# A four-layer graph network on one core: edge searches issued further ahead, and one relational layer's projections cut into small steps

## The chip, the core and the metric

The kernel runs on one core of one Trainium2 chip. Its engines have queues of their own: PE multiplies matrices (with weight loads, PEld, beside it), DVE and ACT work element by element, POOL (GpSimd) here issues gathers, stores and index patterns, SP issues DMAs; ACT can issue DMAs too. An engine executes its queue in order. The metric is the device time of one execution in microseconds.

## The reference

3125 nodes with 128 features, 100,000 edges sorted by target (`dst`), each with a source and one of 8 types. Four networks follow one another; each result is added to its input and normalised by rows.

```python
# L0, three times: D^-1/2 (A + I) D^-1/2 h W, + b, layernorm, relu
deg = segment_sum(ones, row) ; dinv = rsqrt(deg) ; w = dinv[row] * dinv[col]
h = segment_sum(w[:, None] * (h @ W)[col], row) + b
# L1:  segment_sum((x @ W.T + b)[src], dst), own node included
# L2:  (1 + eps) x + segment_sum(x[src], dst), then two linear layers with batchnorm and relu
# L3, two relational layers (128 -> 256 -> 128), relu between:
h = einsum('ni,rio->rno', x, W)
msg = h[etype, src]
sums = segment_sum(msg, dst * 8 + etype) ; cnt = the same of ones
out = (sums / max(cnt, 1)).sum over types + x @ W_root + b
```

## The kernel before

The nodes are 25 blocks of 128. `listed` is the path that runs; `general` stands behind a flag for inputs with too many edges in a node and does not run here. The code is written for a planner that gives each engine its instructions in the order of their place in the program where nothing hinders it, and lets later work go ahead where earlier work still waits by its own estimate; so a line can run long before its place (L309's memset at 1.5 us). Semaphores and the reuse of buffers follow from the tiles: a tile with `bufs=2` makes the third user wait for the first.

**Edges and adjacency (L168 to L301).** Targets, sources and types are loaded as 125 partitions of 800 (L170). Every 200th target is loaded by itself into `smp` (L173), spread over all partitions by a product with ones (L192) and kept in `smb` (L194). The targets as floats go to `dsf` (L181) as 500 rows of 200; source, type and target are packed into one word (`w`, L183 and L185) and go to `pk` (L188). `search(s)` finds for 256 nodes where their edges begin: a coarse count over the samples (L212), a gather `g` of the row of 200 targets (L219), a fine count in it (L224), pointers `ptr` (L228). `keys(s)` gathers 64 packed words for each node (`ew`, L234), splits them (L239 to L249), and transposes them into `kT`. `total(b)` builds one block of the adjacency matrix in four units `u`: one-hot matrices `lo` and `hi` (L161, DVE), sixteen small products into `bld` (L271), an eviction by ACT into `at` (L273). After the four units the identity is added (L277, DVE), `at` is stored to `adj_t` (L278, SP), transposed in four groups through the PSUM tag `mi` (L283), evicted into `av` (L284, ACT), stored to `adj` (L286), and summed over sources by a product with a one-column `onesb` (L290) into two PSUM rows. The loop is written so: `search(0), search(1), keys(0)`, then for each s `search(s+2), keys(s+1), total(2s), total(2s+1)`.

**Passage.** The row sums are copied one row at a time (L312), transposed (L314), and their inverse root is `dinv` (L318 to L322). Then `begin` and `held` (a check) follow. Features `xa` and weights are loaded from the ACT queue, the first network's in a pool that reuses the memory of the edge stage (L473 to L495).

**First network.** `product` (L525 on) runs over seven chunks `CH` of 3 or 4 blocks; in each, five groups of five blocks are loaded (`m`, L514, SP) and multiplied with three bf16 parts of the features (L534). After each group `fill(1.3)` (L536) takes 1.3 steps from the generator `relations()` (L342 on), which counts edges by type (L347, L348, in one step), loads the inverse counts out, gathers the packed words of blocks 14 to 24 edge by edge (`gedge`, L376), makes the indices `gsrc` and keys `gkey` for them, and builds the per-type matrices `rel` of blocks 0 to 13 (56 units of two steps, L429, L448, L455, L457, stores L462 by POOL). A chunk ends with `done`: `times` (L587), bias, layernorm and the split for the next product on DVE and ACT. The second and third network (L569) follow.

**Relational layers.** Blocks 0 to 13 (`DENSE`, four chunks) are done by products with the matrices `rel`: `relation(r, m0, nb, ...)` loads five groups `m8` (L759), casts them (L767 ACT, L769 DVE) and multiplies (L772). After each group, 2.2 steps are taken from `gathered`, which does blocks 14 to 24 edge by edge: a tile of 128 edges is gathered by POOL (`gx`, L806, twelve buffers), one-hot keys `oh` are made by DVE (L798), and three short products per tile add into `ga` (L814); a block has 34 tiles, the last 15: 355. `put` then scales `ga` by the inverse counts. In the first layer `put1` (L875) writes into `z`, and when the chunk of `CH` is complete, `linear1` is called as a whole: transposes (L846), eight products of type weights and a root product for each of two halves (L852, L854), relu by ACT (L855), then for each block two groups of eight products with the second layer's weights (L862), each of which `store3` splits into three bf16 parts (ACT and DVE, L743 to L748) and stores to `ht_d`. `linear1` is also called at the end of each dense chunk. The second layer (L892 on) fetches `ht_d` and works in the same way without `linear1`.

```python
            ahead[0] = -14
            for m0, nb in DENSE:
                z = zp.tile([P, R, 512], F32, name="z", bufs=2)
                for r in range(R):
                    inv = load_inv(r, m0, nb)
                    acc = relation(r, m0, nb, xs, work, 2.2, (0, 1, 0, 1, 0))
                    nc.vector.tensor_mul(z[:, r, : nb * P], acc, inv)
                linear1(z, m0, nb)
            for _ in work:
                pass
```

Of the kernel before, what the change touches and what calls it, by code (L numbers as in the profile page):

```python
# [21 lines left out]
P = 128  # L22
# [4 lines left out]
R = 8  # L27
# [45 lines left out]
def listed(ctx: ExitStack, tc: tile.TileContext, p: dict, out: bass.AP, bad):  # L73
# [11 lines left out]
    onesb = const.tile([P, 1], BF, name="onesb")  # L85
# [5 lines left out]

    def column(name, n=1):
        t = const.tile([P, n], F32, name=f"c_{name}")
        with nc.allow_non_contiguous_dma(reason="a bias"):
            nc.scalar.dma_start(t, p[name].rearrange("(n p) -> p n", p=P))
        return t
# [51 lines left out]
    with ExitStack() as lists, tc.tile_pool(name="f_ps", bufs=1, space=PSUM) as psum:  # L148
# [6 lines left out]
        begin = bg.tile([P, SB, 2], F32, name="begin")  # L155

# [9 lines left out]
        with tc.tile_pool(name="f_t1", bufs=1) as t1:  # L166

            ei = [t1.tile([EP, ET], I32, name=f"e_{n}") for n in ("dst", "src", "edge_type_8")]  # L168
            for t, name in zip(ei, ("dst", "src", "edge_type_8")):
                nc.sync.dma_start(t, p[name].rearrange("(p t) -> p t", p=EP))  # L170
            smp = t1.tile([1, 500], I32, name="smp")
            with nc.allow_non_contiguous_dma(reason="every 200th edge"):
                nc.scalar.dma_start(smp, p["dst"].rearrange("(o i j) -> o i j", o=1, j=200)[:, :, 0])  # L173
# [3 lines left out]
            smf = t1.tile([1, 500], F32, name="smf")  # L177
            nc.vector.tensor_copy(smf, smp)
            df = t1.tile([EP, ET], F32, name="df")
            nc.vector.tensor_copy(df, ei[0])  # L180
            nc.sync.dma_start(dsf.rearrange("(p a) c -> p (a c)", p=EP), df)  # L181
            w = t1.tile([EP, ET], I32, name="w0")
            nc.vector.scalar_tensor_tensor(w, ei[2], 12, ei[1], op0=OP.logical_shift_left, op1=OP.bitwise_or)  # L183
            w2 = t1.tile([EP, ET], I32, name="w1")
            nc.vector.scalar_tensor_tensor(w2, ei[0], 15, w, op0=OP.logical_shift_left, op1=OP.bitwise_or)  # L185
            none = t1.tile([GM, P], I32, name="none")
            nc.vector.memset(none, -1)
            nc.sync.dma_start(pk[:E].rearrange("(p t) o -> p (t o)", p=EP), w2)  # L188
            nc.sync.dma_start(pk[E:].rearrange("(o t) c -> o (t c)", o=GM), none)

            t = psum.tile([P, 512], F32, name="mi", tag="mi", bufs=2)
            nc.tensor.matmul(t[:, :500], ones[0:1, :], smf, start=True, stop=True)  # L192
            smb = t1.tile([P, 500], F32, name="smb")
            nc.scalar.copy(smb, t[:, :500])  # L194
# [9 lines left out]
            fine = t1.tile([P, NC2], F32, name="fine")  # L204
            ptr = t1.tile([P, NC2], I32, name="ptr")
            valid = t1.tile([P, NC2, SL], BF, name="valid")

            def search(s):
# [7 lines left out]
                nc.vector.tensor_copy(irow[:, own], crow[:, own])  # L216
                for c in (2 * s, 2 * s + 1):
# [4 lines left out]
                    )  # L222
                    junk = t1.tile([P, 500], BF, name="junk", bufs=2)
# [6 lines left out]
            def keys(s):  # L230
                own = slice(2 * s, 2 * s + 2)
                ew = t1.tile([P, 2, SL], I32, name="ew", bufs=3)
                for i in range(2):
# [3 lines left out]
                    )  # L237
                f = [t1.tile([P, 2, SL], I32, name=f"f{i}", bufs=2) for i in range(4)]
# [20 lines left out]
            row = [psum.tile([P, 512], F32, name="acc", tag="acc", bufs=2) for _ in range(2)]  # L259
            indp = t1.tile([P, NB, 4], F32, name="indp")  # L260

            def total(b):
                at = t1.tile([P, NB, P], BF, name="at", bufs=2)
                for u in range(64 // PU):
                    lo = t1.tile([P, PU // 2, P, 2], BF, name="lo", bufs=3)
# [10 lines left out]
                    )  # L276
                nc.vector.tensor_add(at[:, b, :], at[:, b, :], identb)  # L277
# [9 lines left out]
                for i in range(7):  # L287
                    w = min(512, NP - 512 * i)
                    q = 32 * (i % 4)
                    nc.tensor.matmul(row[i // 4][q : q + 1, :w], onesb, av[:, 512 * i : 512 * i + w],  # L290
                                     start=(b == 0), stop=(b == NB - 1), skip_group_check=True)

            search(0)
            search(1)
            keys(0)
            for s in range(SB):
                if s + 2 < SB:
                    search(s + 2)
# [1276 lines left out]
```

## Time and profile before

| | us |
|---|---|
| median of 11 runs | 2235.96 (2228.91 to 2243.39) |
| the profiled execution | 2233.91 |
| its span, first to last instruction | 2232.0 |
| busy: PE, DVE, ACT, POOL | 1914.0, 1269.0, 1057.8, 904.8 |
| edges and adjacency | 0 to 293.5 |
| passage | to 312.7 |
| first network | to 732 |
| second and third network | 750 to 946 |
| first relational layer | 957 to 1672 |
| second relational layer | to 2232 |

Times in the profile are microseconds from the span's start. A windows line names a stretch and its length, then the busy time of PE, PEld, DVE, ACT and POOL with the number of instructions, the clock granted to PE (1.00 is full), the DMA engines' busy share and GB/s. A timeline line has start, duration, engine, source line, operation and tiles; in brackets stands the idle time before it and what ended it. "issue" is waiting for nothing that the profile shows. A name with q at its end (ACTq) is the engine's queue issuing a DMA. A waits line reads: waiting instruction <- who released it: total, times, longest. A chain line has start, duration and what was waited for.

### The profile page before, as it was taken

What the parts mean: (1) busy time and instruction counts of PE and PEld (TensorE: products, weight loads), DVE (VectorE), ACT (ScalarE), POOL (GpSimd) and SP (SyncE); (2) the same over time, 40 slices, a digit from 0 to 9 for tenths busy, and PEclk for the clock granted to TensorE, in tenths of its full rate; (3) what the DMA queues carried; (4) which work ended last, traced back from release to release, by engine and by line L of the source; (5) the groups of instructions that cost most, each with busy time, mean ns of one, the idle gap of its engine ahead of it and who ended that gap; (6) DMA issues with size and microseconds to landing.
All of it is one profiled execution on the core that took longest, in us unless ns stands there. A gap on an engine that the chain in (4) does not pass through costs nothing.

```text
span 2232.0 us, 31941 instructions
## 1 busy us (share of the span) xinstructions
PE 1914.0 (86%) x12176; PEld 1383.1 (62%) x12176; DVE 1269.0 (57%) x2303; ACT 1057.8 (47%) x1151; POOL 904.8 (41%) x898
## 2 busy tenths in 40 slices
PE   1676769999999699778997999998879889998994
PEld 1454536666665588656676667567637767776873
DVE  4888889999996563363453445344236344433333
ACT  1776644544442466542232333232327666666760
POOL 3222121121121000027747357437615766666664
PEclk9877679999999899988998999999989999999997
DMA  3444466888887787175655557456539777777762
GB/s 95 182 186 165 173 196 212 269 291 271 268 264 255 232 262 238 45 216 158 168 172 156 169 175 206 136 151 180 145 103 273 219 223 227 195 213 231 202 167 68
DMA packets 384636, 433.06 MB, mean 194 GB/s; under 512 B 28731, under 2 KB 350301, under 8 KB 384472
## 3 DMA queue, kind: packets, MB, share of 16 engines
q1 hardware_dynamic: 314318, 278.95, 40.5%
q0 software_dynamic: 45920, 119.66, 17.6%
q10 hardware_dynamic: 24234, 32.31, 4.9%
q8 instruction: 97, 1.59, 0.3%
q14 instruction: 67, 0.55, 0.1%
HBM read 319.22 MB, written 111.58 MB: 193 GB/s over the span
## 4 chain that ended last, share of the span: by engine, by line
PE 58%; DVE 17%; DMA 9%; issue 8%; ACT 4%; POOL 3%; another core or an unknown queue 1%; ACTq 0%; DVEq 0%; SPq 0%; POOLq 0%
PE acc L772 24%; PE ga L814 7%; PE acc L534 7%; PE acc L569 6%; PE mi L852 4%; PE mi L862 3%; DMA g<-dsf,irow 2%; DVE lo L161 2%; PE bld L448 2%; DVE rhq L161 2%; POOL gx L806 2%; DVE hi L161 1%; DMA back<-ht_d 1%; DVE rlo L161 1%
## 5 line engine op out<-in xcount | busy, mean ns | idle before, releaser
L772 PE MATMUL acc<-m,hilo 128*128 128x384 f32 (+1 forms) x3200 | 776.6, 386 | 43.4 <-issue 27.6
L767 ACT CAST m<-m 128x2560 fp32r<-128x2560 uint8 (+1 forms) x224 | 455.4, 2061 | 444.0 <-PE ga L814 127.6
L772 PEld LDWEIGHTS acc<-m,hilo 128*128 128x128 f32 x3200 | 579.4, 194 | 133.6 <-issue 55.3
L806 POOL DMA_INDIRECT gx<-xt_d,gsrc x355 | 393.5, 1108 | 544.0 <-DMA inv<-inv_d 294.4
L806 POOL DMA_INDIRECT gx<-ht_d,gsrc x355 | 363.9, 1025 | 220.3 <-issue 78.8
L534 PE MATMUL acc<-m,parts 128*128 128x512 bf16 (+1 forms) x1575 | 333.6, 358 | 11.6 <-DMA r_L_gnn_g<-in_L_gnn_g 10.5
L814 PE MATMUL ga<-oh,gx 128*128 128x192 bf16 (+1 forms) x2442 | 265.1, 245 | 65.8 <-issue 34.6
L814 PEld LDWEIGHTS <-gx 128*128 128x128 bf16 x2442 | 177.6, 99 | 157.8 <-issue 121.6
L798 DVE TENSOR_TENSOR oh<-iota,gkey 128x768 bf16<-128x768 bf16 (+1 forms) x188 | 100.2, 534 | 260.8 <-PE ga L814 147.2
L534 PEld LDWEIGHTS <-parts 128*128 128x128 bf16 x1575 | 152.5, 98 | 135.1 <-issue 13.6
L769 DVE CAST m<-m 128x2560 fp32r<-128x2560 uint8 (+1 forms) x96 | 151.6, 1580 | 113.9 <-PE ga L814 43.1
L455 ACT CAST rb<-bld 128x800 uint16<-128x800 f32 x179 | 143.8, 828 | 124.3 <-PE bld L448 119.2
L462 POOL DMA_DIRECT2D rel<-rb x112 | 63.9, 579 | 285.8 <-ACT rb L455 162.7
L569 PE MATMUL acc<-mf,halves 128*128 128x512 f32 (+1 forms) x700 | 155.0, 379 | 17.3 <-ACT mf L566 17.1
L569 PEld LDWEIGHTS acc<-mf,halves 128*128 128x128 f32 x700 | 128.5, 191 | 37.9 <-issue 18.6
L161 DVE TENSOR_TENSOR lo<-iota,kT 128x2048 bf16<-128x2048 bf16 x100 | 121.8, 1218 | 1.5 <-PE bld L271 1.5
L746 DVE TENSOR_TENSOR e<-mi,t 128x512 f32<-128x512 f32 x50 | 34.3, 688 | 136.6 <-ACT t L745 133.8
L566 ACT CAST mf<-m 128x2560 fp32r<-128x2560 bf16 (+1 forms) x42 | 88.2, 2102 | 48.2 <-PE acc L569 38.6
L271 PE MATMUL bld<-hi,lo 128*128 128x50 bf16 x1600 | 75.5, 201 | 40.0 <-DVE hi L161 26.4
L448 PE MATMUL bld<-rhq,rlo 128*128 128x200 bf16 x896 | 107.0, 252 | 1.7 <-DVE rb L457 1.0
L271 PEld LDWEIGHTS <-lo 128*128 128x128 bf16 x1600 | 64.6, 107 | 65.0 <-DVE hi L161 25.6
L448 PEld LDWEIGHTS <-rlo 128*128 128x128 bf16 x896 | 82.5, 98 | 36.1 <-issue 7.8
(230 smaller groups left out, 2102.5 us busy)
## 6 DMA issues: line engine op xcount, KB each, us to landing
m<-rel SPq DMA_DIRECT2D x160, 320.0 KB
rel<-rb POOLq DMA_DIRECT2D x112, 400.0 KB
m<-adj SPq DMA_DIRECT2D x60, 640.0 KB
m<-rel SPq DMA_DIRECT2D x160, 240.0 KB
m<-adj_t SPq DMA_DIRECT2D x40, 640.0 KB
m<-adj SPq DMA_DIRECT2D x45, 480.0 KB
adj_t<-at SPq DMA_DIRECT2D x25, 800.0 KB
adj<-av SPq DMA_DIRECT2D x25, 800.0 KB
```

The source lines that it names most:

```text
L161: nc.vector.tensor_tensor(o, (iota2 if of is None else of)[:, None, :width, :].to_broadcast([P, PU // 2, width, 2]), k[:, :, None, :].to_b ...
L271: nc.tensor.matmul(pt[:, j, : 2 * NB], lo[:, j // 2, :, j % 2], hi[:, j // 2, :, j % 2], start=True, stop=True)
L448: nc.tensor.matmul(pt[:, k, : R * NB], lo[:, j // 2, :, j % 2], hq[:, j // 2, :, j % 2], start=True, stop=True)
L455: nc.scalar.copy(o, src)
L534: nc.tensor.matmul(o, x[:, k, :], m(k - k0), start=(k == 0 and i == 0), stop=(k == NB - 1 and i == 2))
L569: nc.tensor.matmul(acc[:, :w], x[:, 5 * g + k, :], mf[:, k, :w], start=(g == 0 and k == 0 and i == 0), stop=(more is None and g == 4 and k ...
L767: nc.scalar.copy(v, src)
L769: nc.vector.tensor_copy(v, src)
L772: nc.tensor.matmul(acc[:, :w], x[:, 5 * g + k, :], m[:, k, :w], start=(g == 0 and k == 0 and i == 0), stop=(g == 4 and k == 4 and i == 1),)
L798: nc.vector.tensor_tensor(oh[:, : nt // 2], iota2[:, None, : GW * R, :].to_broadcast([P, nt // 2, GW * R, 2]), gkey[:, g, t : t + nt].rear ...
L806: nc.gpsimd.indirect_dma_start(out=gx.rearrange("p i c -> p (i c)"), out_offset=None, in_=table[:], in_offset=bass.IndirectOffsetOnAxis(ap ...
L814: nc.tensor.matmul(acc[:, a:z], gx[:, i, :], oh[:, t % 4 // 2, a - c0 : z - c0, t % 2], start=(a // 512 not in seen), stop=(t == GT[g] - 1 ...
```

## The change

1. **Start.** The target load goes first, alone; the other two wait for it. The samples come out of the float targets by four products with the identity and one product with ones. The packed words wait for the first coarse search. All loads of features, weights and biases go from the ACT queue to SP and wait for the packed store (`later`); they have memory of their own (`f_w`). A square root on ACT at the start loads its table.
2. **Searches.** `search` is cut into `coarse` (count and gather g) and `search` (fine count), the edge fetch is taken out of `keys`; each runs one step further ahead. `total` leaves its second half to `stored`, which runs after two units of the next block. `onesb` has 32 columns, so the row sums stand in 32 equal rows and are copied in three pieces.
3. **relations().** The edge gather comes before the counting, the counting is eight steps, the inverse counts' transposes come last; `fill(1.3)` becomes `fill(1.4)`.
4. **First relational layer.** `linear1` yields after every third type, after each half and after each group of L862. Gathered chunks are `GCH`, whose last is one block. A flag `turn` keeps a dense and a gathered `linear1` apart. The rate is 2.0 for chunks of four blocks, 1.75 for three; two steps are taken at each yield of a dense `linear1`. `z` and `zg` have one buffer each.

```diff
-    onesb = const.tile([P, 1], BF, name="onesb")
+    onesb = const.tile([P, 32], BF, name="onesb")
...
+    nc.scalar.activation(const.tile([P, 1], F32, name="root_eps"), eps_ln, AF.Sqrt)
+    packed = []
+    def later(ld):
+        tc.add_manual_dep(ld.ins, packed[0].ins.name, WAIT, reason="the edges come first")
...
             for t, name in zip(ei, ("dst", "src", "edge_type_8")):
-                nc.sync.dma_start(t, p[name].rearrange("(p t) -> p t", p=EP))
-            smp = t1.tile([1, 500], I32, name="smp")
-            with nc.allow_non_contiguous_dma(reason="every 200th edge"):
-                nc.scalar.dma_start(smp, p["dst"].rearrange("(o i j) -> o i j", o=1, j=200)[:, :, 0])
+                with tc.high_priority():
+                    loads.append(nc.sync.dma_start(t, p[name].rearrange("(p t) -> p t", p=EP)))
+            for ld in loads[1:]:
+                tc.add_manual_dep(ld.ins, loads[0].ins.name, WAIT, reason="the targets come first")
...
+                for i in range(4):
+                    nc.vector.tensor_scalar(smf[:, :, i], ident[:EP, :EP], df[:, 200 * i : 200 * i + 1], None,
+                                            op0=OP.mult)
+                t = psum.tile([P, 512], F32, name="mi", tag="mi", bufs=2)
+                nc.tensor.matmul(t[:, :500], ones[:EP, :], smf.rearrange("p a i -> p (a i)"), start=True, stop=True)
...
-            def total(b):
+            def total(b, behind):
                 at = t1.tile([P, NB, P], BF, name="at", bufs=2)
                 for u in range(64 // PU):
+                    if u == 2 and behind is not None:
+                        stored(*behind)
...
-            search(0)
-            search(1)
-            keys(0)
-            for s in range(SB):
-                if s + 2 < SB:
-                    search(s + 2)
-                if s + 1 < SB:
-                    keys(s + 1)
-                total(2 * s)
-                if 2 * s + 1 < NB:
-                    total(2 * s + 1)
+            near, edges = {}, {}
+            built = None
+            for s in range(-3, SB):
+                if s + 3 < SB:
+                    near[s + 3] = coarse(s + 3)
+                if 0 <= s + 2 < SB:
+                    search(s + 2, near.pop(s + 2))
+                    edges[s + 2] = fetch_edges(s + 2)
+                if 0 <= s + 1 < SB:
+                    keys(s + 1, edges.pop(s + 1))
+                for b in range(max(2 * s, 0), min(2 * s + 2, NB)):
+                    built = total(b, built)
+            stored(*built)
+            tc.add_manual_dep(words.ins, started[0].ins.name, WAIT, reason="the search comes first")
...
-                nc.vector.memset(rs, 0.0)
-                for i in range(4 * g, min(7, 4 * g + 4)):
-                    q, w = 32 * (i % 4), min(512, NP - 512 * i)
-                    nc.scalar.copy(rs[q : q + 1, :w], row[g][q : q + 1, :w])
+                if g == 0:
+                    nc.scalar.copy(rs, leave[0])
+                else:
+                    nc.scalar.copy(rs[:64], leave[1][:64])
+                    nc.scalar.copy(rs[64:96, :P], leave[1][64:96, :P])
...
-                        fill(1.3)
+                        fill(1.4)
...
+    GCH = ((14, 4), (18, 3), (21, 3), (24, 1))
...
                     for r in range(R):
                         nc.tensor.matmul(o[:, :w], w1[:, r, c], z[:, r, :w],
                                          start=(r == 0), stop=False)
+                        if r % 3 == 2:
+                            yield
...
                 if b == m0 + nb - 1:
-                    linear1(zg[0], m0, nb)
+                    while turn[0] == "dense":
+                        yield
+                    turn[0] = "gathered"
+                    yield from linear1(zg[0], m0, nb)
+                    turn[0] = None
...
-            ahead[0] = -14
+            ahead[0] = -12
             for m0, nb in DENSE:
-                z = zp.tile([P, R, 512], F32, name="z", bufs=2)
+                z = zp.tile([P, R, 512], F32, name="z", bufs=1)
                 for r in range(R):
                     inv = load_inv(r, m0, nb)
-                    acc = relation(r, m0, nb, xs, work, 2.2, (0, 1, 0, 1, 0))
+                    acc = relation(r, m0, nb, xs, work, 1.0 * (1.0 + nb / 4), (0, 1, 0, 1, 0))
                     nc.vector.tensor_mul(z[:, r, : nb * P], acc, inv)
-                linear1(z, m0, nb)
+                while turn[0] == "gathered":
+                    next(work)
+                turn[0] = "dense"
+                for _ in linear1(z, m0, nb):
+                    fill(work, 1.0 * 2.0)
+                turn[0] = None
```

## The prediction

> **What bounds the kernel.** First, the page's busy shares in 40 slices (55.8 us each): no engine is full throughout.
>
> ```profile
> PE   1676769999999699778997999998879889998994
> DVE  4888889999996563363453445344236344433333
> PEclk9877679999999899988998999999989999999997
> ```
>
> Slices 1 to 5 (searches, adjacency blocks): DVE at 8, PE lower. Slices 6 to 12 (first network, relation blocks behind it): PE and DVE both at 9. From slice 17 PE leads, with holes. So three stages are read apart. The chain of waits in order of time shows how the first starts:
>
> ```profile
> 0.74 14.34 DMA smp<-in_dst
> ...
> 16.02 8.07 DMA dsf<-df
> ...
> 81.65 4.41 DMA g<-dsf,irow
> ```
>
> The 500 sampled targets take 14.3 us, DVE's next work queues behind them, and one gather g is on the chain in every later step, some 20 us apart. For the loop, from the first one-hot (41.1) to the last block (289.4), the windows and DVE's waits say what is lost (waits: total us, times, longest):
>
> ```profile
> 41.10:289.40 248.30, 171.62 (x2405) 123.63 (x2406) 213.82 (x464) 168.54 (x304) 56.12 (x44) 0.76 0.45 172
> ...
> DVE junk L224 <- DMA g<-dsf,irow: 21.2, 12, 3.5
> DVE at L277 <- ACT at L273: 9.6, 19, 1.1
> ```
>
> DVE works 213.8 of 248.3 us, PE 171.6, ACT 168.5. Nearly all of DVE's idle 34.5 us is those two waits. Then the passage to the first network, ACT in order of time:
>
> ```profile
> 293.52 3.52 ACT L312 COPY rs<-acc 1x512 f32<-1x512 f32 x6
> 297.04 1.28 ACT L318 ACT_TABLE_LOAD   x1
> ...
> 300.95 1.54 ACTq L480 DMA_DIRECT2D w_L_gnn_W<-in_L_gnn_W  x3
> ...
> 311.21 0.75 ACTq L485 DMA_DIRECT2D r_L_gnn_beta<-in_L_gnn_beta  x1
> 312.01 1.55 ACT L501 CAST parts<-v 128x512 bf16<-128x512 f32 x3 [11.57 <-DMA gedge<-pk,gi]
> ```
>
> ACT issues weight loads for 11 us before the cast on which PE's first product (312.7) waits; the releaser printed is not the cause. Last, the two PE stages and PE's waits in the first relational layer:
>
> ```profile
> 345.00:690.00 345.00, 343.09 (x2269) 214.81 (x2269) 337.94 (x612) 171.19 (x247) 59.67 (x105) 1.00 0.80 265
> ...
> 1619.00:1672.00 53.00, 39.87 (x134) 19.34 (x132) 16.29 (x24) 11.29 (x19) 10.21 (x11) 0.87 0.32 97
> ```
> ```profile
> PE ga L814 <- issue: 19.7, 33, 1.7
> PE acc L772 <- issue: 13.8, 25, 1.7
> PE ga L814 <- DMA gx<-xt_d,gsrc: 11.3, 13, 2.7
> PE mi L852 <- DVE z L875: 4.7, 3, 2.2
> ```
>
> **The change, part by part.** The sum is made against the profiled execution, 2233.91 us (span 2232.0); the median, 2235.96, is 0.1% above, so it serves for both.
>
> **Start.** The sample load goes; samples come from the targets' own load. That load's price is not shown alone. One bound: three such loads had landed by 16.1, so (16.1-0.7)/3 = 5.1 us. Other: the lone store of the same 390.6 KB, 8.07. I take 6.6, so targets at 7.3. The float copy (0.56) lets dsf go out at 8.2. The other two loads now go out when the first lands, just ahead of dsf on SP. Alone dsf lands at 16.3; wholly behind both (2x5.1 more) at 26.5; middle 21.4, against 24.1: 2.7 gained. From there to the first one-hot are 17.0 us, of which two gathers of the next step (33.32 to 35.83, 2.5) and its coarse search (2x0.73) now come earlier: 4.0. Against it: words wait for the first search's result. Targets, copy 0.6, four small products (0.23 each, nearest row L277), matmul 2.0, copy 0.6, search 1.9: 13.3. But the two loads land last, at 17.5; plus 2.0 for words and 8.07: packed edges at 27.5, while the first edge fetch is wanted 7.3 after dsf, at 28.7. If dsf is alone, the words bind, and 8 is left of 12. Weights and x now load when packed lands, beside the first gathers: -2. **Start: -5 us (0 to -8).**
>
> By the Trainium skill (DMA: Bandwidth & Descriptors, section "Why a DMA increments its semaphore by 16 and not by 1") a transfer uses the largest number of engines up to 16 that divides its slowest dimension, five for 125 partitions; then dsf queues behind both loads on the same five, and the start would come to about 0 to -2. The 8.07 us for 390.6 KB is in keeping; no run here shows the order.
>
> **Loop.** Gathers go out a step earlier (some 17 us ahead, 4.4 needed), the edge fetch likewise; a block's transposes and store move behind two units of the next, so DVE no longer stands at L277. Removed at most: 21.2+9.6+1.5 (another L277 wait) = 32.3. What binds next is DVE itself, 213.8. PE and ACT, 172 and 169, would then be 80% busy, coupled through two-buffer PSUM; blocks near the end, free of searches, are 7.0 to 7.9 us apart (L277 at 274.4, 282.3, 289.4); DVE's own work is 8.6 a block (213.8/25), so they keep up. The 32-column ones matrix streams the same columns; its load grows from 79 to at most 100 ns, x175 = 3.7 us on PE, which has idle time (if PE bound, 3.7 lost). I take nine tenths: **-29 (-15 to -33).** -15 is half, if each block still waits on ACT.
>
> **Passage.** Seven one-row copies (3.5+0.26) become three (0.58+0.58+0.26), the table load moves to the start (one stands there already, at 3.2). With two transposes of 1.1 and the root, dinv comes 4.4 us after the start at 293.5 instead of 7.1. The 25 loads move from ACT to SP, behind the packed store: at 0.45 each 11 us of SP between 27 and 40, ahead of the first adj_t store (53.65 before, about 48 now); hidden, but 11 us if not. With ACT free, the cast follows dinv by 1.2, and the product's m loads, issued at 300.95 when the old tiles are read, are the next late thing: issued at about 297.3, plus 5 (640 KB at the stage's 235 GB/s is 2.7, plus 2), PE starts at 302.5, not 312.7. **-10 (-4 to -12).**
>
> **First network.** PE is 99% busy, so more relation steps per group (1.4 for 1.3) move work, not the end. Counting is now eight steps: steps before the blocks go from 6 to 16, in all 118 to 128; 118/1.3 = 91 groups of 105 before, 128/1.4 = 91 now. Same end. DVE has the same total, its slack (690 to 732) remains. The edge gather comes ahead of counting, the inv transposes later; inv is first loaded near 985. If the order binds DVE, the counting (8x2.46 = 19.7, partly done in the old idle passage) shows up. **0 (-4 to +15).**
>
> **First relational layer.** 355 tiles at 1.26 us of POOL (0.95 plus 0.30) are 447 us of 712. Fill falls from 2.2 to 2.0 or 1.75 tiles per group: for three blocks POOL needed 2.77 us against PE 2.7, now 2.2 against 2.6. Working through the order: before, 329 tiles are done when the dense part ends, then 26 tiles and a four-block projection follow. Now the three-block chunk's tiles end during the last dense projection, so 18 fill steps do nothing; then come its projection (12 steps), 15 tiles, and one block's projection (8). The 15 tiles are gathered (12 buffers) behind that projection. The tail 1619 to 1672 idles 13.1 of 53 and runs at clock 0.87 (first L852 set 8.9 against 6.2 us: 2.7). Left idle I expect 4. The one block costs more: 64 columns instead of a seventh of 448; 32 weight loads at 0.195 against 1.8 us gives +4.5, nothing if the loads overlap; 2.4 taken. Tail: -13.1-2.7+4+2.4 = -9.4. Mid z waits: 4.7-2.2 = 2.5 off. Start of the gathers (985 to 1040, 16 idle), with 2.0 against 2.2: 2 off. Two small L862 waits (0.9) go. Stalls without a named cause, 33.5 us: I take a tenth off, 3.3, as the order thins. Single z and zg buffers cost nothing: PE reads them in order before the next product ends; if not, one wait of 2.2 per chunk, 8 us. **-18 (-40 to +20).** The second layer stays.
>
> Sum: -5-29-10+0-18 = -62: 2233.9-62 = **2172 us**.
>
> **The rivals.**
> A. *ACT and PE pace the loop.* Each eviction still makes DVE wait, 12 gained instead of 29: 2189. For: PE's bld waits on ACT. Against: the 7.0 us blocks.
> B. *DVE binds the first network*: +19.7, 2192. For: DVE 338 of 345. Against: 42 us of slack after 690.
> C. *The unnamed stalls go too.* PE's 33.5 us, less the 3.3 counted, and about 10 of low clock (0.82 to 0.84 from 1180 to 1220): 2132. For: they lie where short tiles are dense. Against: at 1221 DVE, ACT and POOL are all released by the same unknown queue, which the change does not touch. By the Trainium skill (Runtime: NRT & Kernel Launch, "Instruction fetch mechanics") streaming code past block boundaries is mostly hidden, which would leave order as the cause and favour C; the trace cannot decide that.
> D. *Slower: eviction paces every projection step.* The last L862 groups waited 1.43 us for DVE's e; if all 50 such steps do, split into small steps in PE's fixed order, +71.5 and no gain in this layer: 2233.9-44+71.5 = 2261. It decides from 44/50 = 0.9 us a step. Against: two tiles (0.66) now cover part, and PE ran products meanwhile before.
> E. *No effect*: the planner orders as before: 2234. Against: the buffers and queues themselves change.
>
> **How the numbers follow.** Forecast 0.55, A 0.13, B 0.12, C 0.12, D 0.05, E 0.03. The forecast's own range is 2150 to 2195. Faster by over 0.2% (about what a measurement here can tell from none): 0.55+0.13+0.12+0.12 = 0.92; within: 0.03; slower: 0.05. The range, 2130 to 2208, takes in A, B, C and the start's and passage's bounds.
>
> **What would show it.** Start: first one-hot near 36. Loop: DVE's junk and L277 waits nearly gone, DVE over 94% busy. Passage: no ACT-issued loads, first L534 about 9 us after the last eviction (19 before). Network: still 419 us, PE 99%. Layer: under 10 us idle after the last dense projection. Wrong if the one-hot starts after 41, if DVE still idles 2 us a step, if the network takes over 430, or if L862 waits for e by tens of us.

## The result and the profile after

The changed kernel takes 2176.66 us (median of 8 runs, 2172.17 to 2186.33) against 2234.16 (31 runs): a ratio of 0.9749, 95% interval 0.9733 to 0.9766. The profiled execution has a span of 2176.2 us. The forecast of 2172 holds in the sum, and that is partly luck: four of its terms came out worse by 25.4 us together, three better by 19.2. Stage times, each from the first or last instruction of the lines named in the prediction (the ends of the loop and of the first network are taken, in every run alike, some 0.6 and 0.2 us behind the last instruction's true end, so the stage behind each is as much shorter; differences between runs are not touched):

| stage, us | before | after | difference | forecast |
|---|---|---|---|---|
| start, to the first one-hot | 41.1 | 46.6 | +5.5 | -5 |
| loop, to the end of the last `av` eviction | 253.1 | 230.9 | -22.2 | -29 |
| passage, to the first product | 18.5 | 7.6 | -10.9 | -10 |
| first network | 419.2 | 425.1 | +5.9 | 0 |
| second and third network | 227.6 | 229.8 | +2.2 | 0 |
| first relational layer | 725.7 | 693.8 | -31.9 | -18 |
| second relational layer | 546.8 | 542.4 | -4.4 | 0 |
| sum | 2232.0 | 2176.2 | -55.8 | -62 |

The page of after, busy shares in 40 slices (54.4 us each):

```profile
PE   1666789999999699867999999999999889888994
...
DVE  4989998999996563362444445445345444433333
...
PEclk9877899999999899887999999999999999999996
```

In the loop (slices 2 to 5) DVE stands at 8 and 9 and the clock's dip to 6 is gone; in the first relational layer (slices 18 to 30) PE is at 9 in 11 slices instead of 7. The loop and the first network in the windows view of after (us, then busy PE, PEld, DVE, ACT, POOL, clock, DMA share, GB/s):

```profile
46.60:276.70 230.10, 153.12 (x2433) 112.36 (x2433) 211.39 (x446) 166.05 (x312) 120.37 (x40) 0.84 0.48 187
285.00:710.00 425.00, 418.46 (x2631) 251.86 (x2630) 387.78 (x722) 181.47 (x268) 76.67 (x123) 0.99 0.77 252
```

DVE's work is nearly the same (211.4 for 213.8 us, of which 5.8 and 2.6 already belong to the next stage), its idle time fell from 34.5 to 18.7. POOL, with the same 40-odd gathers, went from 56 to 120 us busy: that is new. What DVE waits for in the loop of after:

```profile
DVE f L288 <- DMA ew<-pk,ptr: 11.6, 5, 3.2
DVE junk L270 <- DMA g<-dsf,irow: 7.0, 5, 3.0
```

The wait for ACT before the identity's add (9.6 us at L277 before, L331 now) is gone; the wait for g fell from 21.2 to 7.0; a wait for the edge fetch is new. The passage, ACT in order of time:

```profile
276.77 0.60 ACT L369 COPY rs<-acc 128x512 f32<-128x512 f32 x1
...
279.90 0.17 ACT L382 ACTIVATE dinv<-mi 128x1 f32<-128x1 f32 x1
...
283.43 1.57 ACT L540 CAST parts<-v 128x512 bf16<-128x512 f32 x3 [3.09 <-DVE v L633]
```

No loads, no table load, and the cast 6.7 us after the first copy instead of 18.5. Last, the first relational layer as a whole, before and then after, windows view:

```profile
959.50:1685.20 725.70, 663.01 (x3323) 466.67 (x3323) 308.98 (x354) 216.16 (x206) 393.62 (x356) 0.96 0.57 163
```
```profile
940.00:1633.80 693.80, 653.53 (x3363) 470.57 (x3363) 312.35 (x355) 221.99 (x214) 388.29 (x357) 0.96 0.61 172
```

PE's idle time fell from 62.7 to 40.3 us and its busy time by 9.5, though it has 40 instructions more. What PE waits for in the layer of after:

```profile
PE ga L858 <- issue: 10.3, 13, 1.8
PE ga L858 <- DMA gx<-xt_d,gsrc: 6.3, 6, 3.3
PE mi L910 <- DVE e L786: 6.2, 7, 1.9
PE acc L819 <- issue: 5.9, 13, 1.7
PE mi L910 <- issue: 5.1, 3, 4.3
```

In before the wait for gathered tiles over the whole layer was

```profile
PE ga L814 <- DMA gx<-xt_d,gsrc: 15.9, 15, 3.6
```

(the 11.3 in the prediction counts from 1000 us on). So issue fell from 33.5 to 21.3 us, gathered tiles from 15.9 to 6.3, the wait for z (4.7) is gone, the one for e is 2.4 longer.

### The profile page after: what moved, and what is told of

The parts are those of the page before. It is cut to its first block, busy times and chain, and to the rows that moved or that the text cites. A ratio compares the mean times of both kernels' runs of the same rounds, so it can differ in the third digit from the quotient of the medians.

```text
span 2176.2 us, 32023 instructions
## 1 busy us (share of the span) xinstructions
PE 1883.7 (87%) x12212; PEld 1370.8 (63%) x12212; DVE 1269.6 (58%) x2303; ACT 1049.8 (48%) x1149; POOL 969.6 (45%) x898
## 5 line engine op out<-in xcount | busy, mean ns | idle before, releaser
L819 PE MATMUL acc<-m,hilo 128*128 128x384 f32 (+1 forms) x3200 | 767.6, 383 | 53.6 <-issue 38.2
L850 POOL DMA_INDIRECT gx<-xt_d,gsrc x355 | 386.8, 1090 | 521.0 <-DMA m<-rel 299.5
L816 DVE CAST m<-m 128x2560 fp32r<-128x2560 uint8 (+1 forms) x96 | 152.1, 1585 | 107.6 <-issue 45.1
L608 PE MATMUL acc<-mf,halves 128*128 128x512 f32 (+1 forms) x700 | 153.9, 377 | 15.9 <-ACT mf L605 15.8
L608 PEld LDWEIGHTS acc<-mf,halves 128*128 128x128 f32 x700 | 128.0, 190 | 35.9 <-issue 17.4
L259 POOL DMA_INDIRECT g<-dsf,irow x26 | 91.7, 3526 | 81.7 <-DVE fine L272 54.6
L910 PE MATMUL mi<-wr,hT 128*128 128x512 f32 x200 | 98.4, 622 | 11.5 <-DVE e L786 6.2
L183 DVE TENSOR_TENSOR rhq<-iota,kT 128x3200 bf16<-128x3200 bf16 x56 | 101.4, 1810 | 0.0
```

Of the source, the lines that this page charges most:

```text
L183: nc.vector.tensor_tensor(o, (iota2 if of is None else of)[:, None, :width, :].to_broadcast([P, PU // 2, width, 2]), k[:, :, None, :].to_b ...
L608: nc.tensor.matmul(acc[:, :w], x[:, 5 * g + k, :], mf[:, k, :w], start=(g == 0 and k == 0 and i == 0), stop=(more is None and g == 4 and k ...
L816: nc.vector.tensor_copy(v, src)
L819: nc.tensor.matmul(acc[:, :w], x[:, 5 * g + k, :], m[:, k, :w], start=(g == 0 and k == 0 and i == 0), stop=(g == 4 and k == 4 and i == 1),)
L850: nc.gpsimd.indirect_dma_start(out=gx.rearrange("p i c -> p (i c)"), out_offset=None, in_=table[:], in_offset=bass.IndirectOffsetOnAxis(ap ...
L910: nc.tensor.matmul(o, hT[:, a, cols(b, 1)], wr[:, a, r : r + 4, :].rearrange("p r c -> p (r c)"), start=(a == 0), stop=(a == 1))
```

## The experiments

The runs form four sets, each on one chip: (1) `late_weights`, `mid_pause`, `two_windows`, `old_layer1`; (2) `after_again`, `gch_old`, `one_block_whole`, `combo`; (3) `before_again`, `no_fill`, `combo3`; (4) `combo4`. `after_again` and `before_again` are single executions. The kernel before takes 2138.1, 2140.2, 2233.3 and 2252.9 us there, so some chips are 4 to 5% quicker for it, and only ratios and stages that agree between chips are compared across sets. (From sets 1 and 2 to the others it is the two relational layers that differ, by some 35 and 55 us; the stages ahead of them agree within 5.) All stages:

| run (set) | start | loop | passage | net 1 | net 2, 3 | layer 1 | layer 2 |
|---|---|---|---|---|---|---|---|
| `after_again` (2) | 45.9 | 235.1 | 7.5 | 424.7 | 229.3 | 660.1 | 486.4 |
| `late_weights` (1) | 37.2 | 241.8 | 7.7 | 426.7 | 229.9 | 659.8 | 480.9 |
| `mid_pause` (1) | 46.5 | 214.4 | 7.7 | 425.0 | 229.5 | 660.6 | 482.7 |
| `two_windows` (1) | 45.4 | 220.5 | 7.5 | 425.2 | 229.6 | 660.5 | 486.8 |
| `old_layer1` (1) | 46.0 | 232.7 | 7.5 | 424.5 | 229.4 | 698.3 | 483.3 |
| `gch_old` (2) | 45.1 | 235.4 | 7.6 | 426.2 | 229.9 | 658.6 | 485.2 |
| `one_block_whole` (2) | 45.8 | 233.7 | 7.6 | 425.3 | 229.9 | 687.6 | 486.6 |
| `combo` (2) | 37.1 | 248.6 | 7.6 | 421.5 | 227.9 | 656.2 | 486.2 |
| `before_again` (3) | 41.3 | 250.6 | 19.0 | 420.2 | 228.9 | 735.4 | 539.8 |
| `no_fill` (3) | 46.4 | 231.9 | 7.8 | 424.5 | 229.3 | 755.4 | 541.3 |
| `combo3` (3) | 37.3 | 223.2 | 7.7 | 421.5 | 228.6 | 694.8 | 542.3 |
| `combo4` (4) | 37.9 | 225.2 | 7.5 | 423.5 | 230.4 | 710.7 | 549.0 |

**The start: `late_weights`.** In after, the targets land early (6.2 us) and the first gather starts at 19.4, yet the one-hot starts late.

```diff
 def later(ld):
-    tc.add_manual_dep(ld.ins, packed[0].ins.name, WAIT, reason="the edges come first")
+    late.append(ld)
...
+for ld in late:
+    tc.add_manual_dep(ld.ins, stores[1].ins.name, WAIT, reason="two blocks come first")
```

> After, with the loads of features, weights and biases held back until block 1's identity is added (about 60 us) instead of until the packed store lands; nothing else changed. Theory S1 (these loads, in flight from 23 to 45 us, slow the first gathers): the first edge fetch lands in about 2.4 us as before instead of 5.7, the first one-hot starts 5 to 8 us earlier than the 46.6 of after, at 39 to 41. Rival S2 (the first block waits because one more step of search is queued ahead of it on POOL and DVE): the fetch is still issued near 30.7 and the one-hot starts at 44 to 46, 1 to 3 us earlier. Either way the third block's store stands behind 11 us of load issues on SP, which may cost the loop up to 8 us once.

Ratio 0.9737 (0.9717 to 0.9756). The start is 37.2: S1, and by more than it said. The queues' shares between 23 us and the first one-hot, in the DMA view of after (packets, MB, share of 16 engines):

```profile
q1 hardware_dynamic: 3735, 2.65, 67.4%
q0 software_dynamic: 426, 0.75, 10.7%
```

and of `late_weights`:

```profile
q0 software_dynamic: 382, 0.65, 16.3%
```

Queue 1 carries the moved loads. They held two thirds of the DMA engines' time while eleven gathers, which DVE waits for one after the other, went through the rest: POOL ends the fourth gather at 24.30 in after and at 24.32 in `late_weights`, and DVE works on it at 28.65 in the one and at 26.07 in the other. But the loop paid the 9 us back: 241.8, where `old_layer1`, with the loop of after on the same chip, takes 232.7. SP in order of time in `late_weights`:

```profile
59.49 0.87 SPq L222 DMA_DIRECT2D xa<-in_x  x1
60.41 3.45 SPq L225 DMA_DIRECT2D xa<-in_x  x1
...
80.16 0.43 SPq L233 DMA_DIRECT2D eps_c<-in_L_gnn_eps  x1
80.69 0.37 SPq L332 DMA_DIRECT2D adj_t<-at  x1
```

The issues took 21 us on SP, not 11, and block 2's store stood behind them; ACT waited 10.8 us for it in one place.

**The loop: `mid_pause` and `two_windows`.** POOL and DVE in order of time in after:

```profile
62.23 0.95 POOL L259 DMA_INDIRECT g<-dsf,irow  x1 [13.55 <-DVE fine L272]
63.48 14.28 POOL L259 DMA_INDIRECT g<-dsf,irow  x1 [0.30 <-issue]
63.62 1.21 DVE L183 TENSOR_TENSOR lo<-iota,kT 128x2048 bf16<-128x2048 bf16 x1
...
76.37 0.56 DVE L183 TENSOR_TENSOR hi<-iota,kT 128x800 bf16<-128x800 bf16 x1
76.86 0.72 DVE L251 TENSOR_SCALAR_CACHE_REDUCE junk<-smb,nid 128x500 bf16<-128x500 f32 x1
...
78.06 0.95 POOL L279 DMA_INDIRECT ew<-pk,ptr  x1 [0.30 <-issue]
```

The second g of a pair lasts 14.28 us instead of 0.95: as long as DVE does nothing but instructions with two inputs in SBUF (`lo`, `hi` and the identity's add, 18 of them). It ends 0.89 us after the first instruction with one input starts. The two edge fetches queue behind it and land when DVE already wants them. Six of the 40 gathers of the loop are caught so, all ending 0.89 to 0.90 us after the start of such an instruction.

```diff
 if u == 2 and behind is not None:
     stored(*behind)
+if u == 2:
+    gap = t1.tile([P, 64], BF, name="gap")
+    seen = t1.tile([P, 1], F32, name="seen")
+    nc.vector.tensor_scalar(gap, hi[:, 0, :32, :].rearrange("p c i -> p (c i)"), 0.5, 0.0,
+                            op0=OP.is_lt, op1=OP.add, accum_out=seen)
```

> After, with one short extra instruction on DVE (64 elements, one input in SBUF, with a sum) between units 1 and 2 of every block, right behind the identity's add; its result is not used. 25 of them at about 0.2 us are 5 us more work for DVE. Theory L1 (POOL's gather cannot run while DVE executes instructions with two inputs in SBUF, back to back): no gather lasts longer than 4 to 7 us (14.3 in after), DVE's waits for g and ew (23.8 us in after) fall under 8, and the loop falls from 230 to 212 to 220 us. Rival L2 (the gathers end late for another reason: their DMA or the order on POOL): gathers still of 14 us, and the loop at 233 to 236.

Ratio 0.9664 (0.9644 to 0.9685), loop 214.4 (232.7 on this chip with the loop of after, in `old_layer1`), longest gather 4.88 us, no wait of DVE's for a gather left: L1. (The 23.8 us in the expectation include two waits of 5.2 ahead of the first one-hot; in the loop of after they are 18.6.) The same gather in `mid_pause`, and the loop in its windows view:

```profile
63.64 4.42 POOL L259 DMA_INDIRECT g<-dsf,irow  x1 [0.30 <-issue]
...
67.17 0.20 DVE L319 TENSOR_SCALAR_CACHE_REDUCE gap<-hi 128x64 bf16<-128x64 bf16 x1
...
68.36 0.98 POOL L279 DMA_INDIRECT ew<-pk,ptr  x1 [0.30 <-issue]
```
```profile
46.00:262.00 216.00, 156.83 (x2440) 116.41 (x2440) 216.00 (x502) 168.58 (x315) 76.98 (x40) 0.86 0.53 201
```

The gather ends 0.89 us after the added instruction starts, though DVE goes on with two-input work right behind it. DVE is busy 216.00 of 216.00 us, 7.7 of them with work of the next stage; more work made the loop 18 us shorter than on the same chip without it.

```diff
+if s >= 0:
+    built = total(2 * s, built)
 if 0 <= s + 2 < SB:
     search(s + 2, near.pop(s + 2))
     edges[s + 2] = fetch_edges(s + 2)
 if 0 <= s + 1 < SB:
     keys(s + 1, edges.pop(s + 1))
-for b in range(max(2 * s, 0), min(2 * s + 2, NB)):
-    built = total(b, built)
+if s >= 0 and 2 * s + 1 < NB:
+    built = total(2 * s + 1, built)
```

> After, with a step's order changed: coarse search of step s+3, block 2s, then fine search and edge fetch of step s+2 and keys of step s+1, then block 2s+1. No work is added; POOL's four gathers of a step come in two pairs. L1 (lock): each pair has a stretch of its own without two-input work, at most half as many gathers are caught and none for more than 7 us; DVE's waits for g and ew under 6 us, period of a step 17.3 to 17.8 us instead of 18.9, loop at 210 to 218 us instead of 230. L2: the loop stays at 228 to 232.

Ratio 0.9669 (0.965 to 0.9689), loop 220.5, just beyond L1's range and far from L2's. But L1's own sign did not come: ten gathers last over 4 us, not half as many as the six of after, and the longest 15.06, not 7. Edge fetches were still caught (3.6 us on average), but their data was wanted later; DVE waited 8.0 us in two places. So this run shows what a gather's place in the order is worth; for the lock itself `mid_pause` is the evidence.

**The first relational layer.**

> After, with the first relational layer's lines of before: projections in one piece, gathered chunks of 4, 3 and 4 blocks, 2.2 tiles a group, z with two buffers in place of z and zg. Everything else as after. If the layer's gain is its own: the stretch from the first product with the relation matrices to the second layer's first product goes from 693.8 us back to 722 to 728, and the time to 2203 to 2210. If half of it came from what the earlier stages leave behind (a different start of the gathers, another clock): 705 to 715.

Ratio 0.995 (0.9936 to 0.9963); the layer took 698.3 us, 38 more than in the other three kernels of the set (28 to 34 had been expected): the gain is the layer's own. PE's wait for gathered tiles in it:

```profile
PE ga L858 <- DMA gx<-xt_d,gsrc: 38.9, 40, 3.8
```

In `mid_pause`, on the same chip, it is 12.9. So 26 of the 38 us are these waits; 7.5 are PE's longer busy time (648.6 against 641.1). The edit has three parts (small steps, fills and their rate, the last single block); sets 2 and 3 try to take them apart.

```diff
-GCH = ((14, 4), (18, 3), (21, 3), (24, 1))
+GCH = ((14, 4), (18, 3), (21, 4))
```

> After, with the gathered chunks of before (4, 3 and 4 blocks, no single last block); steps, rates and buffers as after. Theory P1 (the layer's gain comes mostly from the last chunk's single block, which shortens what stands alone at the end): the layer loses 8 to 15 us of the 38 that the old layer lost against after. Rival P2 (it comes from the projections' small steps and the fills between them): loses 0 to 5 us.

658.6 us, and the same ratio as after, 0.9749 (0.972 to 0.9777): the last single block gives nothing (P2). The opposite, old layer with the new chunks:

> After, with the first relational layer as before (whole projections, no tiles gathered during a dense one, 2.2 tiles a group), but with the gathered chunks of after, the last a single block. P1: the layer is 23 to 30 us longer than after's at most 38, that is, the single block alone gives back 8 to 15. P2: 33 to 38 longer, the single block gives nothing by itself. If both edits are needed together, both this run and the one before it lose more than 15.

687.6, 27.5 more than `after_again` (ratio 0.9873, 0.9849 to 0.9898): within P1's range, but `gch_old` speaks against P1. Beside whole projections the single block gives some 10 us (698.3 in set 1, 687.6 here; the layer of after agrees within 1 us on these two chips), beside stepped ones none. What PE waits for in the layer, first `after_again`, then `one_block_whole`:

```profile
PE ga L858 <- DMA gx<-xt_d,gsrc: 11.6, 16, 2.9
PE mi L910 <- DVE e L786: 2.9, 4, 1.7
```
```profile
PE ga L858 <- DMA gx<-xt_d,gsrc: 32.4, 38, 4.0
```

21 of the 27.5 us are waits for gathered tiles; PE's busy time, 7.7 longer, makes up most of the rest. So it was asked whether the even spread of the gathers is what counts:

```diff
-acc = relation(r, m0, nb, xs, work, 1.0 * (1.0 + nb / 4), (0, 1, 0, 1, 0))
+acc = relation(r, m0, nb, xs, work, 2.5, (0, 1, 0, 1, 0))
...
 for _ in linear1(z, m0, nb):
-    fill(work, 1.0 * 2.0)
+    pass
```

> After, with nothing gathered during the dense projections (their steps run back to back) and 2.5 tiles a group elsewhere so that as many are done by the end; the gathered chunks' projections stay in small steps, the last chunk one block. Theory F (the gain comes from spreading the gathers evenly, so that PE outruns POOL less): PE's waits for gathered tiles rise from 11.6 to 30 us or more and the layer from 660 to 683 to 692. Rival S (it comes from the gathered projections' small steps, which cover for late tiles): waits stay at 10 to 15, the layer at 660 to 668.

The layer took 755.4 us on a chip where `combo3`, with the layer of after, takes 694.8: 61 more, where F said 23 to 32, and the whole kernel is slower than before (1.0084, 1.0051 to 1.0117). The layer of `no_fill` in the windows view:

```profile
939.90:1695.30 755.40, 688.93 (x3363) 488.82 (x3363) 309.75 (x354) 219.83 (x213) 387.55 (x356) 0.92 0.56 158
```

Its waits for gathered tiles, and the largest of its waits for issue:

```profile
PE ga L858 <- issue: 25.8, 44, 1.7
PE ga L858 <- DMA gx<-xt_d,gsrc: 12.5, 11, 3.1
```

F's sign was waits for gathered tiles of 30 us or more. They are 12.5 (8.3 in `combo3`), inside what S said, while the layer's time is far outside S. So neither theory describes this run. What grew against `combo3` is something else: PE is busy 38 us longer for the same 3363 instructions (688.9 for 650.7) and idles 22 us longer, and of that idle time issue, without a visible cause, takes 43.2 us where it took 16.6. PE's granted clock is 0.92 over the layer, 0.96 in after; where it is low, PE also idles:

```profile
989.00:1039.00 50.00, 35.08 (x177) 23.28 (x176) 14.54 (x15) 6.99 (x3) 36.20 (x36) 0.75 0.48 135
...
1189.00:1239.00 50.00, 49.17 (x205) 32.14 (x203) 19.46 (x24) 15.13 (x18) 18.97 (x18) 1.00 0.50 144
```

But idle time alone does not explain the long busy time: the layer of before idles 62.7 us in all, nearly the 66.5 here, and has a clock of 0.96 and 663.0 us of busy time. The small steps of the gathered projections, which this kernel keeps, do not bring the gain by themselves. The run changes two things, no gathers in the dense projections and the higher rate that this needs, and it ran on a chip with issue stalls, while F and S were priced on one without; which part of the layer's edit cures the waits for gathered tiles is left open.

**The chips.** `after_again` is the changed kernel on a quicker chip.

> The changed kernel itself, for stage times beside the next three on one chip. Start 46 to 47 us, loop 229 to 233, passage 7.6, first network 425; if the chip is that of the first four runs, the first relational layer takes 660 us and the second 483 (693.8 and 542.4 in the trace of after).

It came as expected but for the loop: start 45.9, loop 235.1, the layers 660.1 and 486.4.

> The kernel before itself, for its stage times beside the other runs' chips: the median there is 2138 to 2140 us, 95 less than 2234, and after is 2084 to 2091, 87 to 93 less. If PE's idle time put down to issue (33.5 us in the first relational layer of before, as much in the second) belongs to the one chip and not to the order of the kernel's work, it is gone here too: under 5 us in each layer beyond the one 15 us stretch at the start, the layer 690 to 700 instead of 725.7, the second 485 to 495 instead of 546.8. If the order made it, it stays at about 30 in this kernel.

This set ran on a chip where the kernel before takes 2233 us, so its condition did not come up: PE's waits for issue in the layer are there again (18.1, 14.4 and 3.4 us). But `old_layer1` has the layer's old order on a quick chip, and there they are zero but for the one stretch of 15 us ahead of the first product. In the second layer it is the same: after has

```profile
PE acc L819 <- issue: 17.2, 35, 1.2
PE ga L858 <- issue: 16.2, 25, 1.8
```

and `after_again` no wait for issue at all. So it takes the chip to have these stalls. How many there are on a chip that has them goes with the order: 33.5 and 35.9 us in the layer of before; 21.3, 16.6 and 26.7 in after, `combo3` and `combo4`, which share a layer; 43.2 in `no_fill`. Each is one trace.

**Together: `combo`, `combo3`, `combo4`.** (a) and (b) of the expectation are the first two edits below; (c) is four `yield`s ahead of L475.

```diff
 if u == 2 and behind is not None:
     stored(*behind)
+if u == 2:
+    ahead()
...
+for i, ld in enumerate(late):
+    tc.add_manual_dep(ld.ins, stores[1 + i // 2].ins.name, WAIT, reason="a block comes first")
```

> After with three edits. (a) Each of the two coarse counts of a step is done in the middle of a block, behind the identity's add, instead of at the step's start: it is the single-input stretch in which POOL can issue, at no extra work. Lock theory: loop 205 to 212 us (214.4 with the extra instruction, 231 in after); without it 230. (b) The loads of features and weights go out two at a time behind each block's store: contention theory: start at 37 to 39 us (46.6), and the loop does not pay for it (late_weights paid 11); if the features' load disturbs wherever it stands, the loop gains 5 back. (c) Four more yields between the sum over gathered edges and the product that checks it: the first network 419 us (425), if PE's 4.1 us idle there and the lower clock behind it are the cause; 425 if not. In all 2084 - 20 - 9 - 6 = about 2049 on that chip, 0.958 of before.

Ratio 0.9749 (0.9725 to 0.9774), as after. The start (37.1) is as forecast and no g lasts over 1.7 us, yet the loop takes 248.6. DVE's waits in it:

```profile
DVE junk L271 <- DMA g<-dsf,irow: 34.4, 15, 4.4
```

With its count in the middle of block 2s+1, a gather for the very next step has half a block to land, and needs more. So the forecast of 205 to 212 failed on the look-ahead, not on the lock. The first network gained 3.2 us, though PE still waits 2.7 us for the sum (4.2 in `after_again`): about half of what (c) said.

```diff
-built = total(b, built, lambda: half(s + 3, b % 2))
+built = total(b, built, lambda: half(s + 4, b % 2))
```

> The combination again, with the one thing put right that the trace of combo shows (DVE waited 34.4 us for g in 15 places, since its count in the middle of a block left the gather half a block instead of a step): the counts in the middle of blocks 2s and 2s+1 are those of step s+4, not s+3. All else as in combo. Lock theory: DVE idles under 5 us between 46 and 250, a step takes 17.1 to 17.4 us, loop 206 to 212 us; start 37 to 39; first network 421; in all about 2040 to 2048 on that chip, 0.953 to 0.957 of before. If the features' load beside block 2 costs again, up to 5 more.

Ratio 0.9663 (0.9636 to 0.969), where 0.953 to 0.957 had been expected. Steps of 17.07 us (g at 67.61 and 84.68), but a loop of 223.2: past step 9 no count is left to break DVE's runs, fetches of 14.49 and 13.74 us come back, and DVE waits 6.3 us for them.

> combo3 with the short extra instruction of mid_pause in the middle of the last seven blocks, where no count is left to stand there (in combo3 two edge fetches of 14.49 and 13.74 us at 196 and 215 us made DVE wait 6.3 us). Lock theory: no gather over 5 us, DVE's waits for ew and g under 1 us, loop 217 to 220 us instead of 223.2, the time about 5 us under combo3's, 0.961 to 0.966 of before. If those two waits have another cause, the loop stays at 223 to 225.

Ratio 0.9655 (0.9624 to 0.9685), loop 225.2. DVE's waits in the loop of `combo4`:

```profile
DVE lo L183 <- PE bld L331: 7.6, 10, 1.4
DVE at L340 <- ACT at L333: 2.9, 5, 0.9
```

No gather lasts over 4.63 us and no wait for one is left, as the lock theory said; but the loop did not get shorter, and 225.2 is what the rival said. PE and ACT now make DVE wait. `mid_pause` had none of that; whether the loads spread over the loop or the chip (the slowest of the four) makes the difference was not tried. Still `mid_pause`, `combo3` and `combo4` all lie below after, by intervals that do not touch its 0.9733 to 0.9766 and that do not tell the three apart. The simplest of them is one short instruction in after.

## Why the prediction was right or wrong

**Start: wrong in sign.** The data came as forecast or earlier: targets at 6.2 (7.3 said), first gather at 19.4 (21.4). The step that failed is "Weights and x now load when packed lands, beside the first gathers: -2"; it cost 9.4 (46.6 against 37.2 without). Without it the start would have been 3.9 shorter than before, inside the range. A second term failed with it: the gathers and the coarse search that were to "come earlier: 4.0". From the first gather to the first one-hot `late_weights` still needs 17.8 us (19.4 to 37.2), as before did (24.1 to 41.1), since one more step of search now stands ahead of the first block. The packed words bound nothing. The rule of the Trainium skill that the prediction cited (DMA: Bandwidth & Descriptors, "Why a DMA increments its semaphore by 16 and not by 1") is borne out by the trace: from 6.2 to 19.5 queue 1, which carries the two loads and then dsf, takes 26 to 32% of the 16 engines' time, which is about five of them, the second load has landed at 15.54, and dsf is read at 19.4. The 0 to -2 drawn from the rule did not follow, because its price was too high: the three took 13.2 us, not 2x5.1+8.07 = 18.3. In before the three loads had shared the engines with queue 10 (40.7% of their time up to 16.2), and the first packet of dsf moved only at 20.0, 4 us after its issue at 16.02; in after queue 1 has no such gap between 7.0 and 18.2.

**Loop: right in kind, 7 short.** L277's wait went, as said. The step that failed is "Gathers go out a step earlier (some 17 us ahead, 4.4 needed)": issuing is work of POOL's, and one gather in six or seven does not get through beside a run of two-input DVE work, 14 us long now that nothing makes DVE pause. In before the longest gather took 1.85 us: by this reading DVE's own waits had left the gaps, and taking them away closed these. "What binds next is DVE itself" came true only in `mid_pause`.

**Passage: right**, -10.9, by the steps given; dinv came 3.6 us after the first copy (4.4 said) and the cast 3.0 later (1.2 said), because a counting instruction of `relations()` stood ahead of its input on DVE.

**First network: +5.9 for 0.** The step "more relation steps per group (1.4 for 1.3) move work, not the end" missed that PE executes one product of `relations()` (L476) in its order and waits for DVE's sum there: 4.1 us in after, no such wait before. In sum, though, PE idles only 1.8 us more than before in this stage (6.6 and 4.9); the other 4.1 are longer busy time (418.5 and 414.3). `combo`, with four more yields, got 3.2 us back and left 2.7 of the wait. Rival B named DVE's order, at 19.7. The rest, and 2 us in the second and third network, stay open.

**First relational layer: -32 for -18.** The tail came as said (43.0 - 39.4 = 3.6 us of PE idle from 1590 to 1633), but not by the single block, which costs nothing to take out. The mis-sized term is the fill: the prediction saw that "for three blocks POOL needed 2.77 us against PE 2.7, now 2.2 against 2.6" and priced it at 2 us at the start and a tail. On the quick chips the layer's edit is worth 38 us, 26 of them waits for gathered tiles and 7.5 PE's busy time (`old_layer1` against `mid_pause`). On the chip of before and after the 31.9 us are 22.4 of idle time (issue 12.2, gathered tiles 9.6, z 4.7, with 2.4 more at e) and 9.5 of busy time. That the fills and their rate are what cures the waits, and not the small steps, is argued and not shown: `no_fill` was to show it and did not. The size has play, too: the layer of before took 725.7 and 735.4, that of after 693.8, 694.8 and 710.7 on chips with issue stalls.

**Rivals.** A (PE and ACT pace the loop) did not happen in after, and shows up in `combo4`, once the gathers are free. C (the unnamed stalls go) came a third of the way: 21.3 us for 33.5, where a tenth had been counted. The order moves them, as C assumed, but they are a chip's. D fell: PE waits 6.2 us for e at L910, not 71.5. E (no effect) fell with the result.

## What to carry to other kernels

Issuing a transfer early buys little if the engine that issues it is shut out: where POOL issues gathers beside long runs of two-input DVE work, leave DVE a single-input instruction every few microseconds, and place it where work of that kind is due anyway, with the look-ahead counted from there. For loads moved "out of the way", work out what they land beside and each queue they pass: 2 us guessed was 9.4, first on the DMA engines, then on SP. Where one engine feeds another at nearly its own rate, look at what the feeder does while the consumer has other work: with whole projections PE waited 26 us longer for gathered tiles. When a total comes out right, compare its terms: here errors of 25 and 19 us nearly cancelled.

## What the hardware showed that was not expected

**A gather is held by DVE's two-input work.** Alone it takes 0.95 us, held up to 15.06 (`two_windows`). Every gather over 4 us in after and in `mid_pause` ended 0.89 to 0.90 us after the start of a one-input DVE instruction, however short (0.20 us). In the loops of all traces together 84 gathers last over 4 us, none of them in the two of before: 76 end 0.89 to 0.91 us after such a start, and the other eight 0.82 us after DVE falls idle. Not every gather beside such a run is held: others got through in 1.0 to 1.7 us. In after one begun at 85.79 took 1.63 us and one at 160.98 took 13.74, both 0.40 us into a `lo`; what decides is open. DVE's instructions beside held gathers were not longer (1.21 us for `lo` throughout).

The Trainium skill (SBUF — State Buffer, section "SBUF: two separate sides") describes a port pair that DVE and GpSimd share as an exclusive lock, taken by DVE instructions with two SBUF inputs against GpSimd ones that read SBUF, so that the loser blocks. The traces agree on the blocking. They do not show DVE ever being the loser here, and where the page has the lock held for one instruction, the gather of 14.28 us stayed out through 18 in a row.

**Chips differ by 4% on one kernel, nearly all of it in two stages.** In its second relational layer after has 33.4 us of issue waits on PE on one chip and none on another, and that layer takes 542.4 and 486.4 us. On the quicker chip PE waits more for gathered tiles instead (27.2 us for 5.3); its idle time is 36 us less in all and its busy time 20. Why is open.

**PE's idle time and a low granted clock come together, but not one for one.** The same 3363 instructions of a layer kept PE busy 653.5 us at 40 us of idle time and a clock of 0.96, and 688.9 at 66 and 0.92. But the layer of before, with 62.7 us of idle time, has 0.96 as well. Which causes which, no run here shows.
